# Leftover rows of an expert: a third unit of 64 rows beside its first whole slot, in place of half slots of 128 rows

## The chip, the cores and the metric

The kernel runs on one core of a Trainium2 chip. Its five engines are called PE (matrix products; PEld is its loading of the stationary operand), DVE (vector), ACT (scalar functions), POOL and SP; the last two, and ACT, also issue transfers. The metric is the device time of one execution in microseconds (us), as the median of a few runs. Both kernels compute the same function on the same inputs. The time before is 2757.75 us, the median of three runs from 2754.98 to 2759.22.

## The reference

A 1 x 256 x 64 x 64 image passes through three parts. First a group norm and a box-window linear attention (left out here). Then its 4096 positions become tokens of 256 channels, with an eight-head softmax attention over all of them. Last comes a mixture of eight experts, which the change is about:

```python
logits = xt @ Wr + br                                  # xt: 4096 tokens x 256
probs = jax.nn.softmax(logits, axis=-1)
top_p, top_idx = jax.lax.top_k(probs, TOP_K)           # TOP_K = 2 of E = 8
weights = top_p / top_p.sum(axis=-1, keepdims=True)
xn = (xt - mu) * jax.lax.rsqrt(var + LN_EPS)
xe = xn[None, :, :] * ln_g[:, None, :] + ln_b[:, None, :]
h = jax.nn.gelu(jnp.einsum('end,edh->enh', xe, W1) + b1[:, None, :], approximate=False)   # 256 -> 1024
y = jnp.einsum('enh,ehd->end', h, W2) + b2[:, None, :]                                    # 1024 -> 256
sel = jnp.take_along_axis(jnp.transpose(y, (1, 0, 2)), top_idx[:, :, None], axis=1)
out = (weights[:, :, None] * sel).sum(axis=1)
```

Each token needs only its two experts: 8192 rows in all, some 1024 an expert. Everything is fp32.

## The kernel before

The kernel runs the convolutional part, then the attention (16 rounds), then the experts. The work of the experts is cut into *units* of 128 rows of one expert. A *slot* is one pass over one expert's weights: a whole slot has two units (SLOT = 256 rows), a half slot one. The list `usual` names the slots in order: EARLY = 4 slots, one each for experts 0 to 3, with rows from the first ETILES = 12 tiles of tokens, routed ahead during the attention; then NS = 28 whole slots; and after every seventh of these a half slot, four in all. Which expert a slot serves is known only on the chip.

The routing (`route_and_run`, DVE for the most part) counts each expert's rows (`total`, less those `gone` into early slots) and gives it whole slots, and a half slot if at most 128 rows are over (`more`, `size`, `ends`, `begins`). It moves each row to its place (`row`, `rest`), and turns the places into two lists by one-hot products: for every group of eight tiles DVE and ACT make `line` (L1638) and `piece` (L1641, L1644, L1645; as wide as there are units, NU = 72), and PE multiplies them into `back` (L1647). The lists are `source` (which token to gather into a unit's row) and `target` (where its result goes). `owners` (L1591 to L1602) computes the expert of every slot into `expert_of`. Should more units be needed than planned, `more_slots` is set and a branch at L1976 runs the spare units one by one.

`run` executes slots as a pipeline. `load` reads the expert's number into a register of SP (L1354), starts SP's transfers of the weights (W1 and W2, 1 MB each, three buffers; b2 and columns, two) and POOL's indirect gathers of the rows, one for each unit (L1391; four buffers). `enter` transposes the rows on PE (L1405, four transposes for a whole slot) and scales them on DVE (L1414). Then come eight hidden blocks: two products with W1 (`hp`, L1440), with a slot's rows as the moving columns, and GELU on ACT (L1443). The next slot's `enter` follows. Then for each unit eight products with W2 (`yp`, L1457): the unit's rows are the stationary operand, the 256 columns of W2 move. DVE adds the bias (L1461) and POOL scatters the unit to `yrows` in HBM (L1462). Between the steps of the early slots the routing's work is spread with `advance`.

The gathers read `zrows`, the normalised tokens in HBM. ACT scales the last 20 tiles (L1510) between the GELUs of the early slots, and SP stores four at a time (L1514).

The order of the instructions on each engine is set by a planner that knows dependencies and expected durations; within an engine it is then fixed. `issue_after` in the code pins one instruction behind another.

At the end, the rows in `yrows` are read back, weighted, added to the tokens, transposed and stored (L1990 to L2016).

Of the kernel before, what the change touches and what calls it, by code (L numbers as in the profile page):

```python
# [30 lines left out]
P = 128  # L31
# [21 lines left out]
NU = 2 * (NS + EARLY) + NE  # L53
USUAL = 2 * NS + NE // 2
# [11 lines left out]
    "m": {"rank": NE, "iota": P, "before": P, "ones": P, "number": 1, "high": 2 * NT, "base": EARLY, "spare_early": 2 * EARLY, "spare": NU, "unit": NU - NS, "least": 2 * NE},  # L66
# [8 lines left out]
def constants():  # L75
# [35 lines left out]
    out[:, _AT["unit"]] = np.concatenate([2 * np.arange(NS), np.arange(2 * NS, NU)])  # L111
    out[:, _AT["least"]] = 2 * NS * (np.arange(2 * NE) == NE)
# [4 lines left out]
def tile_conv_attn_hybrid(ctx: ExitStack, tc: tile.TileContext, a: dict, out: bass.AP):  # L117
# [1031 lines left out]
    with ExitStack() as phase:  # L1149
# [15 lines left out]
        with (  # L1165
# [164 lines left out]
        of_queries = cutter([qk[:, 0, g, 4 * CH : 7 * CH] for g in range(KC)])  # L1330
        of_values = cutter([v.rearrange("p i c -> p (i c)")])
# [3 lines left out]
            "xe": [of_queries(KC, SLOT) for _ in range(2)],  # L1335
            "b2": [of_queries(C) for _ in range(2)],
            "cols": [of_queries(NH + 2 * KC) for _ in range(2)],
            "hid": [of_values(NH, SLOT) for _ in range(2)],
            "y": [of_values(C) for _ in range(4)],
        }  # L1340
        top = [of_queries(NT) for _ in range(2)]
        source, target = (of_queries(NU, dt=I32) for _ in range(2))
        expert_of = of_queries(NU - NS, dt=I32)
        more_slots = of_queries(1, dt=I32)
# [5 lines left out]
        def weights(slot):  # L1350
            early, *units = slot
            if early is None:
                s = units[0] // 2 if units[0] < 2 * NS else units[0] - NS
                e = nc.values_load(  # L1354
                    expert_of[:1, s : s + 1], engines=(mybir.EngineType.SP,), min_val=0, max_val=NE - 1
                )
                some = lambda z: z[bass.ds(e, 1)]
            else:
                some = lambda z: z[early : early + 1]
# [17 lines left out]


        def run(slots, slot_ps, beside, done, bank):

            def load(slot):
# [4 lines left out]
                rows, n = (lists[:, 0], P * ETILES) if slot[0] is not None else (source, N)  # L1386
                xs = []
                with tc.issue_after(done["moved"]) if "moved" in done else nullcontext():
                    for q in slot[1:]:
                        xs.append(next_of("xs"))  # L1390
                        nc.gpsimd.indirect_dma_start(  # L1391
                            out=xs[-1],
                            out_offset=None,
                            in_=zrows[:n, :],
                            in_offset=bass.IndirectOffsetOnAxis(ap=rows[:, q : q + 1], axis=0),
                        )
                return *of, xs

            def enter(of, by_scalar, tp):

                *_, cols, xs = of
                n = P * len(xs)
                for j in range(len(xs)):
                    for k in range(KC):
                        nc.tensor.transpose(tp[:, k, tok(j)], xs[j][:, tok(k)], ident)  # L1405
                xe = next_of("xe")
                for k in range(KC):
                    gain, shift = (slice(NH + KC * n + k, NH + KC * n + k + 1) for n in range(2))
                    if by_scalar:
                        nc.scalar.activation(  # L1410
                            xe[:, k, :n], tp[:, k, :n], AF.Identity, scale=cols[:, gain], bias=cols[:, shift]
                        )
                        continue
                    nc.vector.tensor_scalar(  # L1414
                        xe[:, k, :n],
                        tp[:, k, :n],
                        cols[:, gain],
                        cols[:, shift],
                        op0=ALU.mult,
                        op1=ALU.add,  # L1420
                    )
# [6 lines left out]
            xe = enter(ahead[0], slots[0][0] is not None, bank().rearrange("p (k n) -> p k n", k=KC))  # L1428
            yield
            (ps,) = slot_ps  # L1430
            for slot, after in zip(slots, [*slots[1:], None]):
                x_now, n = xe, P * len(slot[1:])
# [4 lines left out]
                for m in range(NH):  # L1437
                    hp = ps.tile([P, SLOT], F32, tag="hp", name="ps_hp")
# [11 lines left out]
                if after:  # L1450
                    tp = ps.tile([P, KC, SLOT], F32, tag="tp", name="ps_tp")
                    xe = enter(ahead[0], after[0] is not None, tp)
                to = lists[:, 1] if slot[0] is not None else target
                for j, q in enumerate(slot[1:]):
                    yp = ps.tile([P, C], F32, tag="yp", name="ps_yp")
                    for m in range(NH):
                        product = nc.tensor.matmul(  # L1457
                            yp, hid[:, m, tok(j)], w2[:, m, :], start=m == 0, stop=m == NH - 1
                        )
                    y = next_of("y")  # L1460
                    done["product"], done["y"] = product.ins, nc.vector.tensor_add(y, yp, b2).ins  # L1461
                    nc.gpsimd.indirect_dma_start(  # L1462
                        out=yrows[:, :],
                        out_offset=bass.IndirectOffsetOnAxis(ap=to[:, q : q + 1], axis=0),
# [6 lines left out]
        for s in range(NS):  # L1471
            usual.append((None, 2 * s, 2 * s + 1))
            if s % (2 * NS // NE) == NS // NE:
                usual.append((None, 2 * NS + s // (2 * NS // NE)))
        assert len(usual) == EARLY + NS + USUAL - 2 * NS
        def route_and_run(work_on, slot_ps, beside, done):

            with ExitStack() as experts:
# [16 lines left out]
                with ExitStack() as routing:  # L1495
# [46 lines left out]
                    with tc.issue_after(done["y"]):  # L1542
# [12 lines left out]
                    steps = small.tile([P, N // SLOT], F32, name="steps")  # L1555
                    nc.vector.tensor_scalar(
                        steps, iota[:, : N // SLOT], float(SLOT), float(P), op0=ALU.mult, op1=ALU.add
                    )
# [4 lines left out]
                        steps.unsqueeze(1).to_broadcast([P, NE, N // SLOT]),  # L1563
                        ALU.is_gt,
                    )
                    size = small.tile([P, 2, NE], F32, name="size")
                    nc.vector.tensor_reduce(size[:, 0], more, AX.X, ALU.add)
                    inside = small.tile([P, NE], F32, name="inside")
                    nc.vector.tensor_scalar_mul(inside, size[:, 0], float(SLOT))
                    nc.vector.tensor_tensor(size[:, 1], total, inside, ALU.is_gt)  # L1570
                    nc.vector.tensor_scalar_mul(size[:, 0], size[:, 0], 2.0)
                    ends = small.tile([P, 2, NE], F32, name="ends")
                    nc.vector.tensor_tensor_scan(
                        ends.rearrange("p n e -> p (n e)"),
                        cst["least"],
# [4 lines left out]
                    )  # L1580

                    begins = small.tile([P, 2, NE], F32, name="begins")
                    nc.vector.tensor_sub(begins, ends, size)
                    nc.vector.tensor_sub(begins[:, 1], begins[:, 1], ends[:, 0])
                    nc.vector.tensor_scalar_mul(begins, begins, float(P))
                    nc.vector.tensor_sub(begins[:, 0], begins[:, 0], gone)
                    nc.vector.tensor_add(inside, inside, gone)

                    def owners():

                        past = small.tile([P, NU - NS, 2 * NE], F32, name="past")  # L1591
                        nc.vector.tensor_tensor(
                            past,
                            cst["unit"].unsqueeze(2).to_broadcast([P, NU - NS, 2 * NE]),
                            ends.rearrange("p n e -> p (n e)").unsqueeze(1).to_broadcast([P, NU - NS, 2 * NE]),
                            ALU.is_ge,
                        )
                        owner = small.tile([P, NU - NS], F32, name="owner")
# [3 lines left out]
                        nc.vector.tensor_single_scalar(more_slots, ends[:, 1, NE - 1 :], float(USUAL), op=ALU.is_gt)  # L1602
# [439 lines left out]
```

## Time and profile before

| what | value |
|---|---|
| median of three runs | 2757.75 us |
| profiled execution, its own time | 2761.25 us |
| its span, first to last instruction | 2759.4 us |
| PE busy | 2649.4 us, 96% of the span |
| DVE busy | 1877.0 us, 68% |
| ACT busy | 1511.5 us, 55% |
| POOL busy | 819.3 us, 30% |

By stretch (us from the start of the span), where the experts run:

| stretch | length | PE busy | DVE busy | ACT busy | DMA share |
|---|---|---|---|---|---|
| 2217 to 2281: early slots and routing | 64.00 | 63.18 | 42.35 | 31.52 | 0.51 |
| 2281 to 2339: first usual slots | 58.00 | 58.00 | 7.54 | 15.19 | 0.60 |
| 2339 to 2346.6: a half slot | 7.60 | 7.60 | 0.99 | 2.89 | 0.63 |
| 2346.6 to 2714: other usual slots | 367.40 | 367.40 | 46.70 | 101.33 | 0.59 |
| 2714 to 2760: results read back and stored | 46.00 | 17.48 | 26.29 | 12.56 | 0.82 |

A line of the profile names a line of the code (L1440), an engine, an operation, the tiles it writes and reads, and a shape. In the views of groups the numbers after the bar are busy us and mean ns of one, and then the idle time of the engine just before, with what ended it. In the chain of work that ended last, each line has a start, a length and the work; a time in which no other engine stands between pieces of PE is time that PE alone sets. Matrix products are pipelined: one lasts longer by itself than its step in a row of them.

### The profile page before, as it was taken

The numbers are of one execution on the slowest core, as the hardware profiler recorded it, in microseconds if no ns is written. First come the engines' busy times: TensorE is split into PE (matmuls) and PEld (weight loads), VectorE is DVE, ScalarE is ACT, GpSimd is POOL, SyncE is SP. The second block draws the span as 40 slices with busy tenths as digits, with TensorE's granted clock in tenths as the row PEclk, the third lists the DMA queues.
The fourth block names the chain that finished last, engine by engine and source line by source line (L and its number), as shares of the span: only waits on it lengthen the run. The fifth ranks groups of instructions, "written<-read, shape, count | busy, mean of one in ns | idle before, by whom it ended". The sixth has DMA issues, their size and how long they took to land.

```text
span 2759.4 us, 72312 instructions
## 1 busy us (share of the span) xinstructions
PE 2649.4 (96%) x31106; PEld 1207.4 (44%) x31106; DVE 1877.0 (68%) x2517; ACT 1511.5 (55%) x2111; POOL 819.3 (30%) x919
## 2 busy tenths in 40 slices
PE   6889999997999999999999999999999999999995
PEld 5454336754443556211212121212121278888884
DVE  6758688666878876788888888888888871111114
ACT  3323323222333334899898989898989852222222
POOL 2048677404777752000000010000001122222220
PEclk9999999999999999999999999999999999999997
DMA  5000000000000000455555555555656646665665
GB/s 145 7 23 22 14 26 24 7 13 22 21 15 25 25 22 1 89 117 117 112 114 113 119 112 108 118 114 112 135 112 135 157 142 202 198 220 187 217 202 193
DMA packets 120996, 266.09 MB, mean 96 GB/s; under 512 B 20659, under 2 KB 81817, under 8 KB 106581
## 3 DMA queue, kind: packets, MB, share of 16 engines
q0 software_dynamic: 22368, 133.18, 23.1%
q1 hardware_dynamic: 91124, 119.20, 13.3%
q10 hardware_dynamic: 7168, 8.92, 0.9%
q8 instruction: 248, 4.06, 0.6%
q14 instruction: 88, 0.71, 0.1%
HBM read 127.81 MB, written 18.12 MB: 53 GB/s over the span
## 4 chain that ended last, share of the span: by engine, by line
PE 91%; DVE 3%; DMA 3%; issue 2%; ACT 0%; POOL 0%; ACTq 0%; DVEq 0%; SPq 0%; POOLq 0%
PE ps_three L1747 19%; PE ps_acc L1706 18%; PE ps_sc L822 8%; PE ps_yp L1457 8%; PE ps_hp L1440 7%; PE ps_acc L838 7%; PE ps_sc L722 3%; PE ps_sc L749 3%; PE ps_acc L780 3%; PE ps_two L407 2%; PE ps_two L440 2%; PE ps_mm L1238 2%; DMA yrows<-v,qk 2%; PE ps_two L521 1%; PE ps_acc L768 1%
## 5 line engine op out<-in xcount | busy, mean ns | idle before, releaser
L1747 PE MATMUL ps_three<-qk 32*64 32x512 f32 x6144 | 564.0, 613 | 2.3 <-DVE t L1685 1.3
L1747 PE MATMUL ps_one<-qk 32*64 32x512 f32 x2048 | 557.0, 613 | 0.2 <-ACT pe L1756 0.2
L642 ACT COPY sm<-ps_sc 128x384 f32<-128x384 f32 (+3 forms) x454 | 218.3, 510 | 527.5 <-PE ps_sc L822 338.5
L1779 DVE TENSOR_TENSOR act<-act,pe 128x2048 f32<-128x2048 f32 x195 | 446.8, 2291 | 83.3 <-ACT pe L1759 51.3
L1759 ACT ACTIVATE pe<-ps_three 128x1536 f32<-128x1536 f32 x330 | 477.4, 1447 | 0.0
L649 DVE TENSOR_TENSOR sm<-ps_sc,mask 128x512 f32<-128x512 f32 (+3 forms) x740 | 340.1, 519 | 68.7 <-PE ps_sc L822 65.6
L649 POOL TENSOR_TENSOR sm<-sm,mask 128x192 f32<-128x192 f32 (+3 forms) x428 | 349.8, 847 | 113.6 <-ACT sm L642 113.3
L1779 DVE TENSOR_TENSOR act<-act 128x2048 f32<-128x2048 f32 x150 | 344.9, 2299 | 50.4 <-ACT act L1759 37.3
L1767 POOL DMA_DIRECT2D pe<-pe x108 | 93.1, 862 | 938.3 <-ACT pe L1759 645.7
L1706 PE MATMUL ps_acc<-pe,v 128*32 128x512 f32 x2640 | 352.4, 606 | 0.0
L1443 ACT ACTIVATE v<-ps_hp,qk 128x256 f32<-128x256 f32 (+1 forms) x288 | 132.8, 461 | 344.2 <-PE ps_hp L1440 342.3
L1747 PEld LDWEIGHTS ps_three<-qk 32*64 32x64 f32 x6144 | 112.6, 130 | 415.4 <-ACT pe L1756 243.2
L1759 ACT ACTIVATE act<-ps_three 128x1536 f32<-128x1536 f32 x182 | 263.2, 1446 | 0.0
L1440 PE MATMUL ps_hp<-qk 128*128 128x256 f32 (+1 forms) x1152 | 248.5, 371 | 1.9 <-DMA cstm<-in_constants 1.1
L1457 PE MATMUL ps_yp<-qk,v 128*128 128x256 f32 x1088 | 241.2, 379 | 0.0
L822 PE MATMUL ps_sc<-qk 32*64 32x384 f32 (+3 forms) x3584 | 234.6, 458 | 0.1
L1756 ACT ACTIVATE pe<-ps_one 128x512 f32<-128x512 f32 x330 | 197.3, 598 | 60.3 <-PE ps_one L1747 35.9
L649 POOL TENSOR_TENSOR sm<-sm,ycut 128x384 f32<-128x384 f32 (+4 forms) x146 | 147.2, 1028 | 257.4 <-ACT sm L642 256.9
L1440 PEld LDWEIGHTS ps_hp<-qk 128*128 128x128 f32 x1152 | 195.2, 189 | 48.5 <-ACT v L1443 16.0
L1457 PEld LDWEIGHTS ps_yp<-qk,v 128*128 128x128 f32 x1088 | 203.8, 190 | 26.2
L838 PE MATMUL ps_acc<-sm,v 128*32 128x256 f32 (+3 forms) x2688 | 213.2, 419 | 0.1
L1706 PE MATMUL ps_acc<-act,v 128*32 128x512 f32 x1456 | 193.9, 604 | 0.0
(340 smaller groups left out, 2866.8 us busy)
## 6 DMA issues: line engine op xcount, KB each, us to landing
pe<-pe POOLq DMA_DIRECT2D x108, 1024.0 KB, 7.6
qk<-in_L_ffn_W SPq DMA_DIRECT2D x72, 1024.0 KB
by<-recs SPq DMA_DIRECT2D x48, 256.0 KB
qk<-in_L_ffn_b SPq DMA_DIRECT2D x36, 128.0 KB
rows<-in_x SPq DMA_DIRECT2D x16, 256.0 KB
y<-yrows SPq DMA_DIRECT2D x8, 512.0 KB
y<-yrows ACTq DMA_DIRECT2D x8, 512.0 KB
rec<-recs SPq DMA_DIRECT2D x60, 64.0 KB
```

The costliest lines, as they stand in the source:

```text
L642: copied = nc.scalar.copy(sm[:, :used], sc[:, :used])
L649: done = engine.tensor_mul(to, of, mk.unsqueeze(1).to_broadcast(list(to.shape)))
L822: nc.tensor.matmul(scs[h][u : u + rows, at : at + n], kT[hs[h], P * i + u : P * i + u + rows], qT[hs[h], CH * ix + CELL * c0 : CH * ix + C ...
L838: nc.tensor.matmul(acc[hs[h], CELL * c0 : CELL * c1], v[:, i, hs[h]], sms[h][:, at : at + n], start=not begun[0], stop=last and at == plac ...
L1440: nc.tensor.matmul(hp[:, :n], w1[:, k, tok(m)], x_now[:, k, :n], start=k == 0, stop=k == KC - 1)
L1443: done["gelu"] = nc.scalar.activation(hid[:, m, :n], hp[:, :n], AF.Gelu, bias=cols[:, m : m + 1]).ins
L1457: product = nc.tensor.matmul(yp, hid[:, m, tok(j)], w2[:, m, :], start=m == 0, stop=m == NH - 1)
L1706: nc.tensor.matmul(to[D * hd : D * (hd + 1), :], lhsT(hd), rhs(hd), start=start, stop=stop, skip_group_check=True,)
L1747: nc.tensor.matmul(to[CELL * u : CELL * (u + 1), :], qk[hs, 1, g, P * i + CELL * u : P * i + CELL * (u + 1)], qk[hs, 0, g, chunk(qc)], sta ...
L1756: first = nc.scalar.activation(head(pe, 0), one, AF.Exp, scale=C**-0.5)
L1759: nc.scalar.activation(pe[:, CH:], three.rearrange("p h n -> p (h n)"), AF.Exp, scale=C**-0.5).ins
L1779: latest[:] = [nc.vector.tensor_add(total, total, weights_of[r, i]).ins]
```

## The change

The half slots are dropped. An expert that has up to THIRD = 64 rows over gets a *third unit* of 64 rows beside its first whole slot. Four of the 28 usual slots (positions 0, 7, 14, 21 in `usual`) have room for one; experts with leftover rows take these slots first. In such a slot the hidden products have 320 columns, there are two more transposes (of 64 rows, in a PSUM bank of their own) with two more operations to scale them, and a third yp product of 64 rows, with its own bias add and scatter. The third rows have one buffer, gathered by POOL like the others.

An expert's leftover of 65 to 255 rows makes a whole slot of its own, so that the rule for the number of slots changes, and the plan in the routing with it. Numbering of units changes: thirds are units 0 to 3, slot s has units 4 + 2s and 5 + 2s. NU grows from 72 to 86 (the spare units of the branch at the end, where third units past the fourth and slots past the 28th would go), and with it the one-hot pieces, the lists and the constants. The lists move to the last chunk of the queries' memory.

```diff
+THIRD = 64
+THIRDS = NE // 2
+USUAL = THIRDS + 2 * NS
+NU = THIRDS + 2 * ((2 * N + NE * (SLOT - 1)) // SLOT) + NE - THIRDS
...
+    steps = SLOT * np.arange(N // SLOT)
+    out[:, _AT["steps"]] = steps + np.minimum(steps, THIRD)
...
+            "xs_third": [of_values(C)],
+            "xe": [of_queries(KC, SLOT + THIRD) for _ in range(2)],
...
+            "hid": [of_values(NH, SLOT + THIRD) for _ in range(2)],
...
+        def widths(slot):
+            return [(q, P if j < 2 else THIRD) for j, q in enumerate(slot[1:])]
...
-                    for q in slot[1:]:
-                        xs.append(next_of("xs"))
+                    for q, n in widths(slot):
+                        xs.append(next_of("xs" if n == P else "xs_third")[:n])
...
+                xe = next_of("xe")
+                for first in range(0, len(xs), 2):
+                    some = xs[first : first + 2]
+                    n = sum(x.shape[0] for x in some)
+                    tp = bank().rearrange("p (k n) -> p k n", k=KC)
+                    for j, x in enumerate(some):
+                        m = x.shape[0]
+                        for k in range(KC):
+                            nc.tensor.transpose(tp[:, k, P * j : P * j + m], x[:, tok(k)], ident[:m, :m])
...
-                x_now, n = xe, P * len(slot[1:])
+                x_now, n = xe, sum(n for _, n in widths(slot))
...
-                    hp = ps.tile([P, SLOT], F32, tag="hp", name="ps_hp")
+                    hp = ps.tile([P, SLOT + THIRD], F32, tag="hp", name="ps_hp")
...
-                            yp, hid[:, m, tok(j)], w2[:, m, :], start=m == 0, stop=m == NH - 1
+                            yp[:n], hid[:, m, P * j : P * j + n], w2[:, m, :], start=m == 0, stop=m == NH - 1
...
-        for s in range(NS):
-            usual.append((None, 2 * s, 2 * s + 1))
-            if s % (2 * NS // NE) == NS // NE:
-                usual.append((None, 2 * NS + s // (2 * NS // NE)))
+        for first in range(THIRDS):
+            usual.append((None, THIRDS + 2 * first, THIRDS + 2 * first + 1, first))
+            for s in range(THIRDS + first, NS, THIRDS):
+                usual.append((None, THIRDS + 2 * s, THIRDS + 2 * s + 1))
```

In the routing, on DVE (the plan for each expert, the owners of the slots, and the move of the rows; [P, 8] operands unless named):

```diff
+                    nc.vector.tensor_reduce(wholes, more, AX.X, ALU.add)
+                    nc.vector.tensor_scalar_mul(inside, wholes, float(SLOT))
...
+                    nc.vector.tensor_tensor(thirds, total, inside, ALU.is_gt)
+                    nc.vector.tensor_sub(size[:, 1], wholes, thirds)
...
                     nc.vector.tensor_sub(begins, ends, size)
-                    nc.vector.tensor_sub(begins[:, 1], begins[:, 1], ends[:, 0])
-                    nc.vector.tensor_scalar_mul(begins, begins, float(P))
-                    nc.vector.tensor_sub(begins[:, 0], begins[:, 0], gone)
+                    nc.vector.tensor_sub(begins[:, 1], begins[:, 1], thirds)
...
+                    nc.vector.tensor_scalar(
+                        units_used, slots_used, float(NS), 2.0, op0=ALU.max, op1=ALU.mult
+                    )
...
+                    nc.vector.tensor_sub(to_first, first_slot, others)
+                    nc.vector.scalar_tensor_tensor(
+                        to_first, to_first, float(SLOT), thirds, op0=ALU.mult, op1=ALU.mult
+                    )
+                    nc.vector.tensor_scalar(
+                        to_third, first_slot, float(THIRDS), units_used, op0=ALU.is_ge, op1=ALU.mult
+                    )
+                    nc.vector.tensor_add(to_third, to_third, first_slot)
+                    nc.vector.tensor_scalar(
+                        base, others, float(SLOT), float(P * THIRDS), op0=ALU.mult, op1=ALU.add
+                    )
+                    nc.vector.scalar_tensor_tensor(
+                        to_third, to_third, float(P), base, op0=ALU.mult, op1=ALU.subtract
+                    )
+                    nc.vector.tensor_sub(to_third, to_third, inside)
+                    nc.vector.tensor_sub(base, base, gone)
                     nc.vector.tensor_add(inside, inside, gone)
+                    one_slot = each_expert("one_slot")
+                    nc.vector.tensor_scalar_add(one_slot, gone, float(SLOT))
...
-                        past = small.tile([P, NU - NS, 2 * NE], F32, name="past")
+                        nc.vector.tensor_copy(slot_of[:, :NS], iota[:, :NS])
+                        nc.vector.tensor_scalar_add(full, units_used, float(THIRDS))
+                        nc.vector.tensor_scalar(over, unit[:, :n], full, None, op0=ALU.is_ge)
+                        nc.vector.scalar_tensor_tensor(
+                            late, unit[:, 2 * n :], units_used, over, op0=ALU.subtract, op1=ALU.mult
+                        )
+                        nc.vector.tensor_add(late, late, unit[:, n : 2 * n])
+                        past = small.tile([P, NS + n, 2 * NE], F32, name="past")
...
+                        nc.vector.tensor_scalar_add(full, with_thirds, float(NS - THIRDS))
+                        nc.vector.tensor_tensor(full, full, slots_used, ALU.max)
...
-                    rest = small.tile([P, NE, NT], F32, name="rest")
-                    nc.vector.tensor_tensor(rest, row, by_tile(inside), ALU.is_ge)
-                    nc.vector.tensor_mul(rest, rest, by_tile(begins[:, 1]))
-                    nc.vector.tensor_add(row, row, by_tile(begins[:, 0]))
-                    nc.vector.tensor_add(row, row, rest)
+                    for by, at, to, op in zip(
+                        moved_by, (one_slot, inside), (to_first, to_third), (ALU.is_lt, ALU.is_ge)
+                    ):
+                        nc.vector.tensor_tensor(by, row, by_tile(at), op)
+                        nc.vector.tensor_mul(by, by, by_tile(to))
+                    nc.vector.tensor_add(row, row, by_tile(base))
+                    for by in moved_by:
+                        nc.vector.tensor_add(row, row, by)
```

## The prediction

> **What bounds the kernel now.** I read the page first: the busy rows, then the chain of work that ended last. PE is busy in 96% of the span and carries 91% of the chain. DMA, ACT and DVE are far from full where the change acts.
>
> ```profile
> PE   6889999997999999999999999999999999999995
> ...
> PE 91%; DVE 3%; DMA 3%; issue 2%; ACT 0%; POOL 0%; ACTq 0%; DVEq 0%; SPq 0%; POOLq 0%
> ```
>
> Next the same chain in order of time, around one half slot (start and length in us):
>
> ```profile
> 2331.30 0.22 PE ps_tp L1405 x2
> 2331.51 6.91 PE ps_yp L1457 x32
> 2338.42 0.89 PE ps_hp L1440 x8
> 2339.31 0.11 PE ps_tp L1405
> 2339.42 1.12 PE ps_hp L1440 x8
> ...
> 2343.11 3.46 PE ps_yp L1457 x16
> 2346.57 6.99 PE ps_hp L1440 x32
> 2353.56 0.44 PE ps_tp L1405 x4
> ```
>
> The expert stage is PE from end to end: no piece of another engine stands between. A whole slot takes 6.99 + 0.44 + 6.91 = 14.34 us. Between the yp products of the slots around the half slot lie 2354.00 - 2331.51 = 22.49 us, 8.15 more than a slot, and the slot before had two transposes fewer (0.22). So a half slot costs 7.93 us: 4.25 for hp, 3.46 for yp, 0.22 for its own two transposes.
>
> Then groups by shape in the window 2281:2714, and for one more width the line L1238. An fp32 product appears as two instructions:
>
> ```profile
> L1440 PE MATMUL ps_hp<-qk 128*128 128x256 f32 x896 | 200.3, 382 | 0.0
> L1440 PE MATMUL ps_hp<-qk 128*128 128x128 f32 x128 | 18.2, 285 | 0.0
> ```
>
> ```profile
> L1238 PE MATMUL ps_mm<-act,wqkv x112: 592/592/697, 1027.1 to 1102.7; 128*128 128x512 f32 x112
> ```
>
> A column costs (592 - 382) / 256 = 0.82 ns per instruction, (382 - 285) / 128 = 0.76 on the narrow side.
>
> Last, the place where routing hands over to the usual slots, as a timeline:
>
> ```profile
> 2262.69 0.19 DVE L971 TENSOR_SCALAR qk<-second 128x72 int32<-128x72 f32 x1
> ...
> 2263.38 0.38 SPq L1514 DMA_DIRECT2D zrows<-act  x1
> ...
> 2267.58 0.99 POOL L1391 DMA_INDIRECT qk<-zrows,qk  x1 [16.30 <-DVE v L1461]
> 2268.87 0.97 POOL L1391 DMA_INDIRECT qk<-zrows,qk  x1 [0.30 <-PE ps_hp L1440]
> ...
> 2273.61 0.85 PE L1405 MATMUL ps_tp<-cst,qk 128*128 128x128 f32 x4
> 2274.03 0.20 PEld L1405 LDWEIGHTS ps_tp<-cst,qk 128*128 128x128 f32 x2 [0.24 <-DMA qk<-zrows,qk]
> ```
>
> The list of rows (source, L971) is ready at 2262.9, but the first gather starts at 2267.58: it also needs all of zrows, whose last store is issued only at 2263.38. The release by L1461 that is named there is the later event; the store is the reason I believe. SP was late because it had read expert numbers one by one since 2248.1 (the view of line L1354):
>
> ```profile
> L1354 SPq TENSOR_LOAD <-qk x32: 260/266/877, 2248.1 to 2273.2; - x32
> L1354 SPq FUSED_REGOPS  x32: 147/147/158, 2248.9 to 2273.5; - x32
> ```
>
> A number takes about 0.57 us with gaps, and some 22 of the 32 fit before 2262.6. The gathers then land 0.3 us late for PE. This handover has no slack.
>
> **What the Trainium skill says.** "TensorEngine Tiling (Array Packing)", Key Properties: changing the tiling mode drains TensorE. The trace agrees: eight value products of mode 128*32 take 1.00 us (at 2203.68) between scores of mode 32*64, but 0.86 us (at 2205.54) in the tail, where no score follows. That is 0.14 for that side; sixteen scores take 0.60 + 0.42, against 0.86 for two such sets, so some 0.17 for the other: 0.31 us a round trip. "TensorE: Matmul & The Clock Gate", LDWEIGHTS: its time follows the columns of the stationary operand. The trace agrees (190 ns at 128, 130 at 64), so 64 rows of output do not shorten the stream of 256 columns. "DMA: Bandwidth & Descriptors", Anatomy of one DMA: some 2 us fixed and the bytes after it; the store of 512 KB and its gather, 4.2 us apart, fit. "VectorE: DVE Perf Modes", the errata section: a fixed cost per instruction; the routing's 8-element operations take 0.17 us each, so their number counts.
>
> **The change, part by part.** First whether it computes the same plan. The reference's own routing gives 1063, 1010, 1041, 992, 1033, 995, 1042 and 1016 rows per expert. The early slots take 256 of each of the first four. The rest leaves 28 whole slots and 39, 17, 9 and 18 rows over, at four experts: exactly four half slots before, and four third units and 28 slots after. So neither kernel enters the branch of spare slots.
>
> *Removed*: four half slots, 4 x 7.93 = -31.7 us of PE. With them go 16 SP transfers (8 MB of weights), which no PE wait names.
>
> *Added in the same four places*: hp is 320 wide instead of 256: 64 x 0.82 x 32 instructions = 1.68 us, four times 6.7. The third yp: 16 instructions of 256 columns, 3.46 as in the half slot, 13.8 in all. Two transposes with 64 columns: half of 0.11 each, 0.5 in all. Two changes of mode per third (64 output columns in yp, 64 rows in the transposes): between nothing and 2 x 0.31; I take half, 1.2 in all, as this pair of modes does not occur before. Stage: -31.7 + 6.7 + 13.8 + 0.5 + 1.2 = -9.5 us (-10.7 to -8.2).
>
> *At nothing*: GELU on 320 columns, by its 473 ns at 256 and 367 at 128 some 0.53 us, hides under a 1.08 us pair of products; uncovered it would cost 4 x 8 x 0.05 = 1.7 us. The evacuation of the third transposes hides under the following 10 us of yp; uncovered two operations of about 0.35 us, 2.8 in all. POOL issues as many gathers and scatters as before (60 and 60), and the three scatters of a third slot have 20 us where pairs now have 14.
>
> *Routing, DVE.* Eight more operations on 8 elements at 0.19 (start to start): 1.5. Three more on 128x256 at 0.4: 1.2. NU goes from 72 to 86, so L1641 and L1645 (0.75 each, eight times) grow by 14/72, less the fixed part: 2.2. Owners: seven more small operations and 864 instead of 704 elements in two: 1.7. L1556 (0.9 us at 2217.7) goes, ahead of work that waits for PE at 2232 anyway, and 32 KB more of constants load: nothing. Together 6.6 us on an engine that is busy without a break from 2233 to 2262. The list is ready at about 2269.3 instead of 2262.9. The expert numbers come 4 to 5 us later too, but SP then reads 28 instead of 32, and fewer ahead of the store; I let the store come at the same time or up to 3 us later. First gather: 2269.4 to 2270.2.
>
> *Routing, PE.* The 64 list products (L1647) grow from 144 to 172 columns: eight take 0.51, so 12 ns each, 0.75 us on the path. The early slots' products cover DVE's delay, and end their hp at 2273.7 + 0.75 = 2274.5.
>
> *The new wait.* The first usual slot has a third unit: PE's transposes there wait for three gathers. Issued 1.29 apart from 2269.8 and landing some 5 us later, as the second does now, the third lands at about 2277; the gathers around the handover take 2.8 to 5.9 us, so 2275.5 is possible. Queued behind that wait on PE is the last early slot's yp, and everything after. Stall: 1 to 2.5, less 0.3 paid now: +1.9.
>
> Sum: -9.5 + 0.75 + 1.9 = -6.9 us. The profiled execution, 2761.25 (span 2759.4 and 1.85 around it), would take 2754.4. It lies 3.5 above the median, within the scatter; from the median of 2757.75 the forecast is 2750.9.
>
> **The rivals.** *Free tiling and no late gather*: the modes change at no cost and the third transposes are put behind yp. Then -10.7 + 0.75 - 0.3: 2747.5. For it: 6.9 us of ready yp. Against: yp is behind the transposes in the program and now on PE.
>
> *The handover is 7 us late*: SP reads all 28 numbers ahead of the last store (2252.8 + 28 x 0.57, then store and gathers, third landing near 2281.5). -9.5 + 0.75 + 6.7: 2755.7, no difference to be measured. For it: 22 loads went ahead of the store before. Against: a store ready earlier than the loads may go first.
>
> *Slower*: the third gather stands in POOL's queue behind the scatters of the last early slot (2283.03 and 2286.23 before, each waiting for the one before to land). Then it lands after 2290, and PE, with no other work, loses every us of it; 14.3 us (8.8 gained and 5.5 for the bound) is where it turns. Price near that: 2763.5. For it: gathers and scatters alternate in POOL's queue there. Against: they stand in the order of the slots, and the third belongs to the first one.
>
> *The change does not do what it says*: another expert over a multiple of 256 makes a fifth third; expert 7 has 1016 rows, 9 short. Then 26 single units run, at least 26 x 7.93 = 206 us: 2957. The counts speak against it.
>
> **How the numbers follow.** My forecast 55%, of which 40 lie below 2752.2 and 15 above; free tiling 18%; late handover 18%; slower 7%, spare slots 2%. A measurement of this kernel tells some 0.2% (5.5 us) from no change. Faster: 40 + 18 = 58%; same: 15 + 18 = 33%; slower: 9%. The range goes from just under free tiling to just over the late handover, 2746.3 to 2756.8; the forecast's own is 2748 to 2754.
>
> **What would show it.** Right: 64 instead of 72 weight loads; a third slot of 14.34 + 5.4 to 6.0 us in the chain; L1440 with 320 columns near 434 ns; PEld or PE ps_tp waiting 1 to 3 us on a gather just ahead of the first usual slot; the list ready near 2269. Wrong: whole slots that lengthen, a wait on PE for weights or GELU in a third slot, or the attention stage changing its length, which I take as fixed.

## The result and the profile after

In 15 runs each, the kernel after took 2751.3 us (median; 2747.3 to 2754.7) and the kernel before 2756.5 (2751.5 to 2760.3). The ratio is 0.9982 with a 95% interval of 0.9974 to 0.9990: 5.0 us faster (2.8 to 7.2), 0.18%, just inside the 0.2% that I had set as the bound for no change. The forecast of 2750.9 is half a microsecond away. That is luck in part: the kernel before came out 1.2 us lower over 15 runs than over the three from which the forecast was counted, and the gain is 5.0 us where it was to be 6.9. The parts of the sum are compared below.

The profiled execution after takes 2754.69 us, its span is 2752.9. First the page, its busy row of PE and the shares of the chain that ended last:

```profile
PE   6889999997999999999999999999999999999995
...
PE 91%; DVE 3%; DMA 3%; issue 2%; ACT 0%; POOL 0%; ACTq 0%; SPq 0%; DVEq 0%; POOLq 0%
```

Nothing has changed at this scale. The stages say more. I cut each trace at four instructions of PE: the first hp product of the experts, the counts' product in the routing, the first hp of a usual slot, and the end of the last yp product. Each trace is one execution.

| us | before | after | difference |
|---|---|---|---|
| start to first hp | 2216.96 | 2213.61 | -3.35 |
| early slots to the counts | 15.07 | 15.00 | -0.07 |
| routing (counts to first usual hp) | 49.18 | 51.66 | +2.48 |
| usual slots | 432.66 | 424.08 | -8.58 |
| tail (last yp to the end) | 45.57 | 48.52 | +2.95 |

The first row is scatter between executions: two experiments on the kernel before, with its code ahead of the experts, have 2212.40 and 2210.11 there, and the kernels derived from the one after have 2207.31 to 2212.48. So each edit has to be read from the later stages. The transposes of the first usual slot, and the yp products behind them, still lie in the routing stage by this cut.

**Usual slots.** The chain in order of time around the first slot with a third unit (start and length in us, engine, tile, line):

```profile
2272.62 0.70 PE ps_tp L1420 x6
2273.32 7.10 PE ps_yp L1467 x32
2280.43 8.61 PE ps_hp L1450 x32
2289.04 0.44 PE ps_tp L1420 x4
2289.48 10.51 PE ps_yp L1467 x48
2299.99 7.19 PE ps_hp L1450 x32
2307.18 0.44 PE ps_tp L1420 x4
2307.61 6.91 PE ps_yp L1467 x32
2314.52 6.99 PE ps_hp L1450 x32
```

Against a plain slot (6.99 and 6.91, as in the last two lines): hp +1.62, yp +3.60, the yp ahead +0.19 and the hp behind +0.20; the transposes ahead take 0.70 instead of 0.44. Together 5.87 us for a third, where a half slot took 7.93. Of the first third, 0.45 us (transposes and the yp ahead) falls into the routing stage. Groups by shape, in the window 2281:2707:

```profile
L1467 PE MATMUL ps_yp<-qk,v 128*128 128x256 f32 x896 | 198.3, 379 | 0.0
L1450 PE MATMUL ps_hp<-qk 128*128 128x320 f32 x126 | 34.6, 432 | 0.0
L1420 PE MATMUL ps_tp<-cst,qk 128*128 128x128 f32 x108 | 16.2, 273 | 0.0
L1467 PE MATMUL ps_yp<-qk,v 128*64 128x256 f32 x64 | 14.7, 382 | 0.0
L1420 PE MATMUL ps_tp<-cst,v 64*128 64x64 f32 x6 | 1.0, 247 | 0.0
```

At 320 columns an hp instruction takes 432 ns, where I had 434. The third's yp takes 382 ns with half the output columns, a full one 379.

**The handover.** The timeline around it:

```profile
2258.80 0.41 SPq L1525 DMA_DIRECT2D zrows<-act  x1
...
2263.86 0.20 DVE L975 TENSOR_SCALAR qk<-second 128x86 int32<-128x86 f32 x1
...
2266.37 0.99 POOL L1401 DMA_INDIRECT qk<-zrows,qk  x1 [3.01 <-DVE v L1471]
...
2268.93 0.92 POOL L1401 DMA_INDIRECT v<-zrows,qk  x1 [0.31 <-issue]
...
2272.46 0.60 PE L1420 MATMUL ps_tp<-cst,qk 128*128 128x128 f32 x4
...
2272.99 0.33 PE L1420 MATMUL ps_tp<-cst,v 64*128 64x64 f32 x2
```

Counted from the counts' product, the list is ready 4.6 us later than before (35.45 against 30.85) and the first gather is issued 2.2 us later (37.76 against 35.55). Yet no transpose names a wait, not even the third's: its gather, issued at 2268.93, was there when PE came at 2272.99.

**Routing.** PE lost its time earlier. The timeline where it stood still, behind the second group of list products:

```profile
2246.02 1.05 DVE L1638 TENSOR_TENSOR past<-slot_of,ends 128x864 f32<-128x864 f32 x1
...
2247.66 1.04 DVE L1645 TENSOR_REDUCE owner<-past 128x54 f32<-128x864 f32 x1
...
2248.68 0.87 DVE L1693 TENSOR_TENSOR piece<-which,units 128x688 bf16<-128x688 bf16 x1
2249.58 0.87 ACT L1696 ACTIVATE piece<-piece,cstm 128x688 bf16<-128x688 bf16 x1 [1.18 <-DVE piece L1693]
...
2250.36 0.46 ACT L1453 ACTIVATE v<-ps_hp,qk 128x256 f32<-128x256 f32 x1
...
2250.86 0.70 PE L1450 MATMUL ps_hp<-qk 128*128 128x256 f32 x2 [1.32 <-ACT v L1453]
```

Read upwards: PE waits 1.32 us for a GELU (before, 0.36 us for one). The GELU stands on ACT behind a copy of a piece, which waited 1.18 us for DVE's piece, and that stands on DVE behind the owners' operations.

**The tail.** Here is what POOL does at the branch that skips the spare units, listed by source line, in the kernel after:

```profile
L2030 POOLq EVENT_SEMAPHORE  x4: 17/43/43, 2712.2 to 2712.5; - x4
L2030 POOLq COMPARE_BRANCH  x1: 55/55/55, 2709.6 to 2709.6; - x1
L2030 POOLq INC_SWDGE_SEM  x1: 792/792/792, 2712.6 to 2712.6; - x1
```

and in the kernel before:

```profile
L1978 POOLq EVENT_SEMAPHORE  x4: 17/43/43, 2719.0 to 2719.2; - x4
L1978 POOLq COMPARE_BRANCH  x1: 50/50/50, 2718.8 to 2718.8; - x1
```

Before, POOL's next instruction starts 0.14 us after the branch has ended; after, 2.60 us. The read back of yrows follows POOL's mark behind it: it starts 9.10 us after the last yp, against 6.39.

So the theory with which I went into the experiments was: -8.6 from the usual slots, +2.5 from the routing (width of lists and the owners), +2.5 from the skipped branch. That makes -3.6, within the measured interval. The experiments change the last two parts of it.

### The profile page after: what moved, and what is told of

It is laid out like the page before. It is cut to its first block, busy times and chain, and to the rows that moved or that the text cites. A ratio compares the mean times of both kernels' runs of the same rounds, so it can differ in the third digit from the quotient of the medians.

```text
span 2752.9 us, 71916 instructions
## 1 busy us (share of the span) xinstructions
PE 2638.8 (96%) x30978; PEld 1189.6 (43%) x30978; DVE 1880.4 (68%) x2534; ACT 1502.6 (55%) x2079; POOL 820.5 (30%) x919
## 4 chain that ended last, share of the span: by engine, by line
PE 91%; DVE 3%; DMA 3%; issue 2%; ACT 0%; POOL 0%; ACTq 0%; SPq 0%; DVEq 0%; POOLq 0%
PE ps_three L1799 19%; PE ps_acc L1758 18%; PE ps_sc L826 8%; PE ps_yp L1467 7%; PE ps_hp L1450 7%; PE ps_acc L842 7%; PE ps_sc L726 3%; PE ps_sc L753 3%; PE ps_acc L784 3%; PE ps_two L411 2%; PE ps_mm L1242 2%; PE ps_two L444 2%; DMA yrows<-v,qk 2%; PE ps_two L525 1%; PE ps_acc L772 1%
## 5 line engine op out<-in xcount | busy, mean ns | idle before, releaser
L1453 ACT ACTIVATE v<-ps_hp,qk 128x256 f32<-128x256 f32 (+1 forms) x256 | 122.8, 480 | 342.8 <-PE ps_hp L1450 338.5
L1467 PE MATMUL ps_yp<-qk,v 128*128 128x256 f32 (+1 forms) x1088 | 241.7, 380 | 0.0
L1450 PE MATMUL ps_hp<-qk 128*128 128x256 f32 (+1 forms) x1024 | 236.8, 389 | 2.8 <-ACT v L1453 1.7
L1467 PEld LDWEIGHTS ps_yp<-qk,v 128*128 128x128 f32 (+1 forms) x1088 | 200.3, 187 | 30.7 <-issue 1.3
L1450 PEld LDWEIGHTS ps_hp<-qk 128*128 128x128 f32 x1024 | 180.7, 189 | 52.7 <-ACT v L1453 13.6
```

Source lines behind the costliest of these rows:

```text
L1450: nc.tensor.matmul(hp[:, :n], w1[:, k, tok(m)], x_now[:, k, :n], start=k == 0, stop=k == KC - 1)
L1453: done["gelu"] = nc.scalar.activation(hid[:, m, :n], hp[:, :n], AF.Gelu, bias=cols[:, m : m + 1]).ins
L1467: product = nc.tensor.matmul(yp[:n], hid[:, m, P * j : P * j + n], w2[:, m, :], start=m == 0, stop=m == NH - 1)
```

## The experiments

### What a third and a half cost, and the changes of mode

`x1_no_thirds`, on the kernel after: the third units' products and transposes go.

```diff
-            usual.append((None, THIRDS + 2 * first, THIRDS + 2 * first + 1, first))
+            usual.append((None, THIRDS + 2 * first, THIRDS + 2 * first + 1))
```

> The kernel after, with its four third units' work left out (their slots have two units, hp is 256 wide; the 83 leftover rows get other results). Theory: a third costs PE 5.87 us in the chain (hp +1.62, transposes +0.26, yp +3.60, and +0.39 in the two neighbours), so the usual stage falls by 4 x 5.87 = 23.5 us, from 424.1 to 400.6 us, and the time to 2751.3 - 23.5 = 2727.8 us. Rival, the prediction's half price of the mode changes: 4 x 5.55 = 22.2 us, stage 401.9. If the third gather at the handover costs anything that the chain doesn't show, the routing stage falls under 51.7 us too, by up to 1.9; I expect no fall there by more than 0.3.

`x2_no_halves`, on the kernel before: the half slots go.

```diff
-            if s % (2 * NS // NE) == NS // NE:
-                usual.append((None, 2 * NS + s // (2 * NS // NE)))
```

(The diffs here are cut to the lines that matter. In both of these a scatter of a result that is there anyway takes the place of the one left out.)

> The kernel before, with its four half slots left out (products, weights and gathers; the 83 leftover rows get other results). Theory: a half slot costs PE 7.93 us, so the usual stage falls by 31.7 us, from 432.7 to 401.0 us, and the time from 2756.5 to 2724.8 us. Rival: half slots cost more than their own products, by what stands around them (weights that come faster, buffers): then the stage falls by over 33 us. Either way the stage should end at the length of the kernel after without thirds (400.6), since both are then 28 whole slots and nothing else, within 0.5 us.

`x4_full_mode`, on the kernel after: the third unit in full width, with buffers to match.

```diff
-                        xs.append(next_of("xs" if n == P else "xs_third")[:n])
+                        xs.append(next_of("xs" if n == P else "xs_third"))
...
-                            yp[:n], hid[:, m, P * j : P * j + n], w2[:, m, :], start=m == 0, stop=m == NH - 1
+                            yp, hid[:, m, tok(j)], w2[:, m, :], start=m == 0, stop=m == NH - 1
```

> The kernel after, with the third units' transposes and yp products at the full 128 rows and columns (hid has room for 384; rows 64 and up of a third unit are left over from earlier and are not stored), so that PE never changes its tiling mode there. Theory: two round trips of mode cost 0.68 us a third slot, and the fuller transposes give back 0.11, so a third slot falls from 20.2 to about 19.6 us and the usual stage from 424.1 to 421.8 us; time 2749. Rival: the extra 0.68 us isn't mode but the wait for hid, or weight loads: then the stage stays or grows by 0.4 (424.1 to 424.5).

| | usual slots, us | routing, us | time, median us | ratio to before |
|---|---|---|---|---|
| x1_no_thirds | 400.95 | 51.20 | 2729.4 | 0.9909 (0.9892 to 0.9925) |
| x2_no_halves | 400.95 | 49.39 | 2726.0 | 0.9893 (0.9877 to 0.9910) |
| x4_full_mode | 421.99 | 51.43 | 2750.6 | 0.9982 (0.9974 to 0.9990) |

The ratios, here and below, are to runs of the kernel before that were made beside each kernel; for the experiments their medians lie between 2753.1 and 2755.8 us.

Without thirds and without halves the stage has the same length to 0.01 us, so the difference between the kernels in it is made of these units: 31.71 us for four halves (7.93 each), and 23.13 us for the thirds. To the thirds belongs the part of the first one that the cut puts into routing: there `x1_no_thirds` is 0.46 us shorter than the kernel after, more than the 0.3 that I had allowed, and its chain has 0.44 and 6.91 us where the kernel after has 0.70 and 7.10. That makes 23.59 us for four thirds, 5.90 each: the theory's 5.87, not the 5.55 of half price for the modes.

In full mode the usual stage is 2.09 us shorter than in the kernel after, and routing, with the entry of the first third, 0.23 us: 2.32 in all, 0.58 for a third. Twice the work in its transposes takes 0.11 of it away again (an estimate, half of the 0.22 us that the two take in full width), so that no change of mode is worth 0.69 us a third, two round trips of some 0.35. The theory had 0.68. The chain of `x4_full_mode`:

```profile
2268.62 0.66 PE ps_tp L1420 x6
2269.27 6.91 PE ps_yp L1467 x32
2276.18 8.61 PE ps_hp L1450 x32
2284.79 0.44 PE ps_tp L1420 x4
2285.23 10.36 PE ps_yp L1467 x48
2295.59 6.99 PE ps_hp L1450 x32
```

The yp of 48 products takes 10.36 instead of 10.51, the neighbours are back at 6.91 and 6.99, and the hp is still 8.61. The whole time shows no gain over the kernel after: its interval reaches 2.2 us to either side. The stage shows it: it has 424.08 or 424.09 us in three of the four whole kernels that keep the narrow third (after, x5, x7; x6, with 425.04, is told below), and 421.99 in all three that don't (x4, x8, x9).

### What the width of the lists costs, and the owners

`x3_wide_before`, on the kernel before: room for 86 units.

```diff
-NU = 2 * (NS + EARLY) + NE
+NU = 2 * (NS + EARLY) + NE + 14
```

> The kernel before with room for 86 units instead of 72, so that its lists, pieces, list products, list of constants and its skipped branch of spare units (26 instead of 12) are as wide as those of the kernel after; half slots and owners stay as they were. Theory A, width: the list products grow by 0.75 us (0.60 us for eight instead of 0.51) and DVE's pieces make PE wait some 0.3 to 0.7 more, so routing goes from 49.2 to between 50.1 and 50.7 us, not to 51.7, since the owners' extra operations are missing. Theory B, all of the +2.5 us comes from the width: 51.5 or more. Tail: 48.5 us if the skipped branch's length delays the read back, 45.6 if not. The usual stage stays at 432.7.

`x5_owners_late`, on the kernel after: the owners' block two groups later.

```diff
-                            if n == 0 and i8 == G:
+                            if n == 0 and i8 == 3 * G:
```

> The kernel after, with the owners' block (eleven operations on DVE, 3.7 us of them in the two large ones and what stands among them) put behind the fourth group of eight tiles instead of the second. In after PE waits 1.32 us for a GELU that stands in ACT's queue behind a piece copy, which waits for DVE's piece, which stands behind the owners; x4 shows the same 1.3. Theory A, place: the stall goes and routing falls from 51.66 to about 50.3 us; the time falls by 1.3, to about 2750. Theory B, total of DVE's work: the stall only moves to the fourth group and routing stays within 0.4 of 51.66. Against both, a new wait is possible: the expert numbers come 4 to 5 us later, and PE would wait on the weights of the first usual slot; then PE ps_hp waits on a DMA there and routing grows by over 1 us.

`x6_narrow_lists`, on the kernel after: lists over 60 units (and the slices to match).

```diff
-                    NPC = NU
+                    NPC = USUAL
```

> The kernel after, with lists, pieces and list products only over the 60 units that are always run; the lists of the 26 spare units are left out, which nothing reads with this data. The products' 64 move from 172 to 120 columns: eight take about 0.43 instead of 0.60 us, 1.4 us in all, and DVE's pieces fall from 0.87 to about 0.63 us, some 3.8 us in 16. Theory A (width makes most of the loss): the stall on the GELU goes too, and routing falls from 51.66 to between 48.9 and 49.5 us. Theory B (the stall comes from the owners alone): 1.4 less, 50.2. Time 2749 to 2750. Tail as in after.

| | routing, us | PE's waits named there | time, median us | ratio to before |
|---|---|---|---|---|
| before | 49.18 | GELU 0.4 | 2756.5 | 1 |
| after | 51.66 | GELU 1.3, piece 0.2 | 2751.3 | 0.9982 (0.9974 to 0.9990) |
| x3_wide_before | 50.63 | piece 0.8, GELU 0.3 | 2760.4 | 1.0015 (1.0008 to 1.0023) |
| x5_owners_late | 51.74 | third gather 0.8, piece 0.4 | 2749.9 | 0.9979 (0.9971 to 0.9988) |
| x6_narrow_lists | 50.30 | piece 1.6 | 2750.1 | 0.9980 (0.9972 to 0.9987) |

Width alone makes 1.45 of the 2.48 us: theory A. Another 0.46 is the first third's own work (`x1_no_thirds`). The 0.6 that is left falls to the owners and the operations that are new in the plan, by difference. `x3_wide_before` is also slower as a whole than the kernel before, clear of no change.

`x5_owners_late` was meant to settle whether the owners' place makes the stall, and gave half an answer. The stall on the GELU went, so their place does make it. But the routing got no shorter, because the wait that my prediction had put at the handover now appeared. Its timeline:

```profile
2265.51 0.97 POOL L1401 DMA_INDIRECT qk<-zrows,qk  x1 [0.30 <-issue]
2268.05 1.00 POOL L1472 DMA_INDIRECT yrows<-v,lists  x1 [1.57 <-issue]
2269.36 0.93 POOL L1401 DMA_INDIRECT v<-zrows,qk  x1 [0.30 <-issue]
...
2271.97 0.31 PE L1420 MATMUL ps_tp<-cst,v 64*128 64x64 f32 x2 [0.81 <-DMA v<-zrows,qk]
```

The third gather now stands behind a scatter of an early slot in POOL's queue: the order of POOL changed with the place of the owners. PE had it 2.6 us after its issue.

In `x6_narrow_lists` routing is 1.36 us shorter than after, the number of theory B, but not by its reasons. The products take 0.49 instead of 0.60 us for eight, 0.9 in all, where I had expected 1.4 from them. And the stall did not stay on the GELU: PE waits 1.6 us for a piece of the third group instead, and in the chain that piece stands on DVE behind the owners' operations (`past` and `owner`), as the GELU did in the kernel after. Its usual slots took 425.04 us, 0.96 more than after; these lie in pauses of 0.14 to 0.28 us in single slots, for which the trace names no cause.

### The skipped branch

`x7_short_branch`, on the kernel after: 12 spare units instead of 26.

```diff
-            for _ in run([(None, q) for q in range(USUAL, NU)], [ps], [], {}, one_bank):
+            for _ in run([(None, q) for q in range(USUAL, USUAL + 12)], [ps], [], {}, one_bank):
```

> The kernel after, with 12 instead of 26 spare units in the branch that this data skips (14 spare units' code is left out; nothing else differs). In the four kernels with 26 POOL's next instruction behind that branch comes 1.7 to 2.6 us after it, in the two with 12 it comes after 0.14 us, and the read back of yrows waits for POOL's mark there. Theory: with 12 it is 0.14 to 0.2 us again, the read back starts 6.2 to 7.0 us after the last yp product instead of 9.1 (8.2 in x4), and the time falls by 1.6 to 2.5, from 2751.3 to about 2749. Rival: the delay comes from something else (DMA traffic, the place of the code), and stays over 1.5 us. Usual stage and routing as in after, 424.1 and 51.4 to 51.7.

POOL's lines at the branch of `x7_short_branch`:

```profile
L2030 POOLq EVENT_SEMAPHORE  x4: 17/43/43, 2703.6 to 2703.9; - x4
L2030 POOLq COMPARE_BRANCH  x1: 50/50/50, 2703.4 to 2703.4; - x1
```

The gap is 0.14 us again, the read back starts 6.79 us after the last yp (9.10), and the time is 2748.3, ratio 0.9975 (0.9964 to 0.9985). The intervals of this ratio and of the kernel after overlap; the gap does not come near. Over all traces it is 0.14 us in the three with 12 units to skip (before, x2, x7), and 1.71 to 2.66 in the seven with 26 in one branch (after, x1, x3, x4, x5, x6, x8). In `x3_wide_before`, where nothing else at the end is new, it is 1.81. What POOL does in the gap the trace doesn't show. That it fetches the instructions that lie behind the jump is my guess, and wasn't tested.

What the gap is worth in the end is less than its 2.5 us. The tail, from the last yp to the end, is 47.17 us in `x7_short_branch`, 1.35 less than the 48.52 after, though the read back starts 2.31 us sooner; and in `x3_wide_before` it is 46.62, 1.05 more than the 45.57 before, where I had expected 48.5 or 45.6 (its gap grew by 1.67 us, but POOL came to the branch 0.63 us sooner after the last yp). What lies behind the start of the read back is not steady: 39.2 us before, 39.4 after, 40.4 in x7 and 41.2 in x2, with the same code there. So the branch accounts for 1.0 to 1.4 us of the 2.95 in the tail, by single traces; the rest stays open.

### Together

`x8_late_third`: full mode as in x4, owners as in x5, and the third's transposes behind the first yp.

```diff
-                for first in range(0, len(xs), 2):
+                firsts = (0,) if xe is None else range(2, len(xs), 2)
+                xe = next_of("xe") if xe is None else xe
+                for first in firsts:
...
+                    if after and j == 0:
+                        enter(ahead[0], after[0] is not None, tp_bank, xe)
                     yield
```

> The kernel after with three edits: full mode as in x4, owners behind the fourth group as in x5, and the third unit's transposes put behind the first yp product of the slot before instead of ahead of it. Theory (the third gather is late at the handover as soon as PE no longer loses time at the GELU; 6.9 us of yp cover it): the 0.8 us that PE waited on v<-zrows in x5 go, routing falls from 51.7 to between 50.7 and 51.0 us, the usual stage is 422.0 as in x4, and the time is 0.9966 to 0.9970 of before. Rival (DVE's total work sets the end of routing): PE waits elsewhere, routing stays at 51.4 or more, time 0.9973.

`x9_two_branches`: x8, with the spare units in two branches.

```diff
+        for some in (range(USUAL, (USUAL + NU) // 2), range((USUAL + NU) // 2, NU)):
+            with (
+                tc.If(more > 0),
```

> The kernel x8, with the 26 spare units in two branches of 13 after each other, on the same condition. Theory (what is jumped over has to be near): POOL goes on 0.14 us after each of the two branches instead of 1.7 to 2.6 after the one; the second branch costs a load, a compare and the marks once more, some 1.3 us on POOL. Net 0.4 to 1.3 us less than x8, tail 46.5 to 47.5. Rival (the marks cost more than the jump): the same or up to 1 us more than x8.

The chain of `x8_late_third` at the handover:

```profile
2263.05 6.91 PE ps_hp L1451 x32
2269.96 0.44 PE ps_tp L1421 x4
2270.40 3.46 PE ps_yp L1468 x16
2273.85 0.22 PE ps_tp L1421 x2
2274.07 3.46 PE ps_yp L1468 x16
2277.53 8.61 PE ps_hp L1451 x32
```

The wait on the third gather is gone, routing is 50.64 and the usual slots 421.99 us, as the theory had it. In these stages it is 3.1 us ahead of the kernel after (1.02 and 2.09). The whole time doesn't show that gain: 2746.3 us is 0.9976 of the kernel before beside it (0.9965 to 0.9987), no better than `x7_short_branch` with 0.9975, and short of the 0.9966 to 0.9970 that I had expected; the rival's 0.9973 is as near. The interval overlaps that of the kernel after.

The two branches cost more than they save. POOL goes on 0.14 us after the first and 1.05 us after the second, though both skip 13 units, and the marks come twice; the read back starts 9.41 us after the last yp instead of 8.36, the tail is 50.23 us instead of 48.09, and the time is 2748.8 (0.9982, 0.9975 to 0.9988). The rival had the direction, and up to 1 us of loss; in the tail it is 2.1.

## Why the forecast was right, and which of its steps were not

- **Half slots removed, -31.7.** Shown: 31.71 in `x2_no_halves`.
- **Added work in the stage, +22.2.** It is 23.6 (`x1_no_thirds`). hp (1.62 for 1.68) and the third yp (3.46) held. The term that was mis-sized is "two changes of mode per third ... I take half, 1.2 in all": `x4_full_mode` shows 0.69 a third, 2.8 in all, a little over the upper bound of 2.5. The price that I had read in the attention, 0.31 a round trip, was near the 0.35 of a pair of modes that doesn't occur there. That changing the tiling mode drains TensorE, as the Trainium skill has it ("TensorEngine Tiling (Array Packing)", Key Properties), agrees with `x4_full_mode`; the price has to be paid in full. And 14.34 + 5.4 to 6.0, given as a sign for a third slot, does not follow from these terms, which make 5.3 to 5.9; it took 5.87.
- **"At nothing": GELU and the evacuation of the third.** Right: no wait in the chain of a third slot.
- **List products, +0.75.** 0.60 instead of 0.51 for eight, as I had it.
- **"The new wait", +1.9: this step failed.** The list came 4.6 us later, where the terms added up to 6.6; the first gather came 2.2 us later, inside my 1.8 to 2.6; but the gather's time to land was taken from a row of before with "some 5" us, and here the third was there within 4.1 us of its issue, in `x5_owners_late` within 2.6. And PE ended its early hp 1.5 us later than I had reckoned, 1.0 of it at the GELU (1.32 for 0.36 before). That I had not seen: I wrote that the early slots' products "cover DVE's delay". They cover it at the end, but inside the routing PE's own GELU waits on ACT behind a copy that DVE feeds. So 1.0 was paid in another place. The two stand in for each other: with the GELU's stall gone, 0.8 us of the predicted wait came (`x5_owners_late`), and went when the third's transposes were put behind yp (`x8_late_third`).
- **Routing in sum, +2.65 forecast, +2.48 measured.** The agreement is partly luck: 0.46 of the 2.48 is the first third's own work, which the forecast has in its stage. Of the 2.0 that are left to compare, +0.75 held and the rest has another cause.
- **The tail, left out of the sum.** "NU goes from 72 to 86" was followed into the lists and the constants, not into the branch that is never entered. It starts POOL's mark 2.5 us later; 1.0 to 1.4 us of that reach the end (`x3_wide_before`, `x7_short_branch`). The tail as a whole grew by 2.95 us in the two traces, the largest term that I missed, and more than half of it has no shown cause.

Step by step the stages give -8.58 + 2.48 + 2.95 = -3.15 us where I had -6.9; measured are -5.0 (-7.2 to -2.8), and the start of the programs scatters by more than routing and tail together make. By medians the forecast was met, by its parts it was some 3.7 us too hopeful: 1.4 in the modes and the rest of the added work, 2.95 in the tail, less 0.6 in the routing. I gave 58% to a gain over 0.2% and 33% to no difference that can be told; the measured 0.18% falls to the second.

Of the rivals, free tiling is out (`x4_full_mode`: two round trips cost 0.69 us a third). The late handover by SP is out: the last zrows store went at 2258.80, after 10 of the 28 numbers. The slower one, a gather behind an early slot's scatter in POOL's queue, does not occur in the kernel after, but `x5_owners_late` has it, for 0.8 us. No spare slot ran.

## What to carry to other kernels

When a change makes a table wider, follow the width to everything that is sized by it, the code that is skipped included; here a branch that isn't entered held up the read back by 2.5 us and the end by 1.0 to 1.4, out of 8.6 that the usual slots gained. When an engine becomes later, look not only for who waits for its result at the end, but also for what shares a queue with its intermediate results: ACT's queue, with a GELU behind a copy, carried DVE's delay to PE. And when stages are cut by an instruction, ask which work of the next stage lies ahead of the cut: here 0.46 us of a third looked like routing. The narrower product saved nothing here, 382 ns over 256 moving columns for 379, and cost its change of mode: filling the tile with rows that nobody reads was 0.58 us cheaper a slot.

## What the runs showed of the hardware

- A yp product with 64 output columns takes 382 ns, with 128 it takes 379, both over 256 moving columns. A round trip of the tiling mode between 128x128 and 64 columns or rows costs some 0.35 us in fp32: around the third's yp 0.15 (10.51 for 10.36) and 0.20 (7.19 for 6.99), and two of them 0.69 in a third slot.
- POOL's first instruction behind a taken branch starts 0.14 us after it when 12 units of code are jumped over (three traces), and 1.7 to 2.7 us when there are 26 (seven traces); behind the second of two branches with 13 units each, 1.05 us. The cause stays open.
- Two kernels with quite different code around them (`x1_no_thirds`, `x2_no_halves`) have the same 400.95 us for 28 slots, while the whole times of one kernel scatter by 7 us.
